# Moving transposes, a row broadcast and additions of rows and diagonals from engines to DMA in a four-layer graph network kernel

## The chip, the cores and the metric

The kernel runs on one core of a Trainium2 chip. The metric is the device time in microseconds (us) of one execution of the whole kernel. The profile shows these engines: PE (TensorE, matrix products; PEld is its weight load), DVE (VectorE), ACT (ScalarE), POOL (GpSimd) and SP (SyncE, which issues DMA transfers). A matrix product in float32 shows as two passes in the profile, a transposition by TensorE as one.

## What is computed

32 independent graphs, each with 512 nodes of 256 features, go through four layers. Each layer aggregates over the graph's own 512x512 adjacency matrix, applies dense weights, adds its input and normalises each row (layer norm).

```python
# layer 0
h = (1.0 + eps) * x + einsum('bnm,bmd->bnd', adj, x)
x = layernorm(x + relu(h @ W1 + b1) @ W2 + b2)
# layer 1
h = einsum('bnm,bmo->bno', adj, x @ W.T + b)
x = layernorm(x + where(h > 0, h, alpha * h))
# layer 2
h = layer_norm(x, gamma, beta)
conv = einsum('bij,bjh->bih', adj, h) @ W_rel + b_rel + h @ W_root
x = layernorm(x + (x + relu(conv)))
# layer 3
h = (epsilon * x + einsum('bnm,bmd->bnd', adj, x)) @ W1 + b1
h = silu(h * rsqrt(mean(h * h, axis=-1) + 1e-6) * rms_weight)
x = layernorm(x + h @ W2 + b2)
```

The hidden width is 512 in layer 0 and 1024 in layer 3. All values are float32.

## The kernel before

*How the work is laid out.* A graph's features lie in a tile of 128 partitions (the nodes, in four chunks) by 4 x 256. Aggregation gives its result with features on the partitions and nodes along the row (`aT`), which is what the dense layers need. Large products are done by a scheme of seven products instead of eight (`seven`), so each has sums of blocks before it (`left_sums`, `right_sums`), done by VectorE, and sums of results after it (`take`, `put`). The sums of adjacency blocks are made once for each graph and used by all four layers.

*The self term.* Layers 0 and 3 add (1 + eps) x or epsilon x. The kernel adds a multiple of the identity (`loop0`, `loop3`, 128x128) to the diagonal blocks of the adjacency matrix and of two of its sums: four places (`self.loops`) of 2 x 128 columns. `sums` (line 650) copies the four blocks aside (`self.plain`, by two-dimensional DMA moves, `carry`), `with_loops` (671) writes block plus loop back with VectorE, and `restore` (667) moves the kept blocks back for layers 1 and 2.

*Bias rows.* `plus_row` (874) adds a 256-wide row to each of the four chunks of x in layers 0 and 3: four additions on GpSimd each time.

*Transposition in layer 2.* `layer2` (935) needs h with features on the partitions. It takes eight 128x128 transpositions on TensorE against an identity (`flip`, 477) into two PSUM banks and copies them to SBUF (lines 938 to 943).

*RMS factors in layer 3.* `column_sums` (793) adds the squares over the hidden width for each node; GpSimd raises to the power -0.5 (`inv_sqrt`, 513). The factor of each node must lie along the row on all 128 partitions, to multiply hT. Four `flip`s of the broadcast column write it to a PSUM bank `pr` (lines 975 to 977), and VectorE multiplies each of eight chunks by `pr` (981).

*What sets the order.* The kernel records every operation with its possible engines and assumed durations (`Plan.do`, `Plan.move`), then walks through them with a list planner (`Plan.order`, 317), which chooses an engine where two are allowed and writes out one fixed order for each engine. All 32 graphs are in this one list; up to `FLIGHT` = 4 are open at once, so that TensorE works on one graph while another waits. Each engine then runs its own list strictly in order. Since every operation is issued by two helper functions, the profile puts line 266 beside all computing and line 280 beside all DMA; groups are told apart by tile names: `room` is one of 36 work tiles of 128 x 1024, `few` one of 12 small ones, `ps` a PSUM bank, `A` a sum of weight blocks, `ident` the identity. All DMA is issued from SP.

```python
        pr = bank(N)
        for c in range(NC):
            flip(pr[:, c * P : (c + 1) * P], rstd[:, c : c + 1].spread(P, P))
```

Of the kernel before, what the change touches and what calls it, by code (L numbers as in the profile page):

```python
# [14 lines left out]
P = 128  # L15
Q = 32
# [10 lines left out]


def in_psum(x):
    return isinstance(x, Part) and x.room.pool.psum  # L30
# [35 lines left out]
def gpsimd_time(n):  # L66
    return 0.15 + n * 0.0024, 0.05


def power_time(n):  # L70
    return 0.37 + n * 0.158, 0.04
# [4 lines left out]
ISSUE, ADVANCE, AFTER, LANES = 0.45, 1.5, 0.35, 8  # L76
# [18 lines left out]
RULES = [(50, 2, last, near) for last in (12, 20) for near in (0, 0.5, 1)]  # L95


class Pool:


    def __init__(self, tiles, grain, spare, psum):
        self.tiles, self.grain, self.spare, self.psum = tiles, grain, spare, psum
        self.clear()

    def clear(self):
        self.rooms = [None] * len(self.tiles)

    def free(self):

        return sorted(  # L110
            (0.0 if r is None else r.until, i)
            for i, r in enumerate(self.rooms)
            if r is None or not r.left
        )


class Room:


    def __init__(self, pool):  # L120
        self.pool = pool
        self.uses = 0
        self.clear()

    def clear(self):
        self.index = None
        self.left = self.uses
        self.until = 0.0


class Part:
# [34 lines left out]
    def place(self):  # L166
        v = self.room.pool.tiles[self.room.index]
        for step in self.steps:
            v = step(v)
        return v  # L170
# [3 lines left out]
class Op:  # L174

    graph: int
    rank: tuple
    ways: dict  # L180
    port: set
    yields: bool
    kbytes: float
    rooms: list = field(default_factory=list)
# [6 lines left out]
class Plan:  # L191
# [10 lines left out]
    def grains(self, x):  # L202
        part = isinstance(x, Part)
        key, ap = (x.room, x.model) if part else (x.tensor.name, x)
        grain = x.room.pool.grain if part else P
        starts = [ap.offset % ap.ap[0][0]]
        dims = list(ap.ap)[1:]
        for step, n in dims[:-1]:
            starts = [s + step * i for s in starts for i in range(n)] if step else starts
        step, n = dims[-1]  # L210
        return {
            (key, g)
            for s in starts
            for g in range(s // grain, (s + step * (n - 1)) // grain + 1)
        }

    def add(self, ways, out, ins, ordered=None, port=(), kbytes=0):
        me = len(self.ops)
        op = Op(self.graph, (self.graph, me), ways, port, "scalar" in ways, kbytes)
        self.ops.append(op)  # L220
        before, results = set(), set()
        writes = self.grains(out) if out is not None else set()
# [22 lines left out]
    def do(self, out, *ways, ordered=None, scrap=None):  # L245
# [3 lines left out]
        port = set()  # L249
        for e, method, _, args, kw in ways:  # L250
            tiles = [x for x in (*args, *kw.values()) if isinstance(x, (bass.AP, Part))]
            ins += tiles
            if e == "gpsimd" and kw.get("op") != ALU.pow or e == "vector" and not (
                method.startswith("bn_") or any(in_psum(x) for x in tiles)
            ):
                port.add(e)

        def issue(engine, method, args, kw):
# [14 lines left out]
            out, ins, ordered, port,  # L273
        )

    def move(self, out, src, kbytes, inward=True):


        def issue():
            self.nc.sync.dma_start(*(x.place() if isinstance(x, Part) else x for x in (out, src)))  # L280

        self.add(
            {"sync": ((ISSUE, ADVANCE + wire_time(kbytes) + AFTER), issue)},
            out if inward else None, [src] if isinstance(src, Part) else [], kbytes=kbytes,
        )
# [31 lines left out]
    def order(self, period, pace, last, near):  # L317
# [15 lines left out]
        oldest, port, wire, lanes = 0, 0.0, 0.0, [0.0] * LANES  # L333
        can_start = {i for i, n in enumerate(behind) if not n}
        done = []
        while can_start:
# [4 lines left out]
            def rooms_free(op):  # L341

                count = {}
                for r in op.rooms:
                    if r.index is None:
                        count[r.pool] = count.get(r.pool, 0) + 1
                at = 0.0
                for pool, n in count.items():
                    if pool not in room_at:
                        room_at[pool] = pool.free()  # L350
                    n += pool.spare[min(op.graph - oldest, len(pool.spare) - 1)]
                    if op.graph - oldest >= self.flight or n > len(room_at[pool]):
                        return None
                    at = max(at, room_at[pool][n - 1][0])
                return at

            best = {}
            for i in can_start:
                op = self.ops[i]
                wait = rooms_free(op)  # L360
                if wait is None:
                    continue
                if op.kbytes:
                    wait = max(wait, lanes[0])
                at = {
                    e: max(free[e], wait, ready[i][e], port if e in op.port else 0.0)
                    for e in op.ways
                }
                way = min(at, key=lambda e: at[e] + sum(op.ways[e][0]) + (YIELD if op.yields and e == "vector" else 0.0))
                best.setdefault(way, []).append((at[way], rank[i], i))  # L370
# [10 lines left out]
            if op.kbytes:  # L381
                wire = max(wire, t + ADVANCE) + wire_time(op.kbytes)
                end = wire + AFTER
                lanes = [*lanes[1:], end]
            if engine in op.port:
                port = end
            for r in op.rooms:
                if r.index is None:
                    r.index = r.pool.free()[0][1]
                    r.pool.rooms[r.index] = r  # L390
# [16 lines left out]
def tile_gnn_stack(ctx: ExitStack, tc: tile.TileContext, a: dict, out: bass.AP):  # L407
# [36 lines left out]
    FLIGHT, ROOMS, SMALL = 4, 36, 12  # L444
# [3 lines left out]
    psum = ctx.enter_context(tc.tile_pool(name="psum", bufs=1, space=bass.MemoryType.PSUM))  # L448
    plan = Plan(nc, FLIGHT)

    def pool(kind, name, n, size, grain, spare):
        return Pool(
            [kind.tile([P, size], F32, tag=f"{name}{i}", name=f"{name}{i}") for i in range(n)],
            grain, spare, kind is psum,
# [3 lines left out]
    rooms = pool(work, "room", ROOMS, NC * D, P, (0, 4, 6, 8))  # L458
# [5 lines left out]

    def gpsimd(method, n, *args, **kw):
        return "gpsimd", method, gpsimd_time(n), args, kw
# [22 lines left out]
    def both(method, o, x, y, engines):  # L489
        plan.do(o, *(e(method, span(o), x, y) for e in engines))  # L490

    def add(o, x, y, *engines):
        both("tensor_add", o, x, y, engines or (vector,))

    def sub(o, x, y, *engines):
        both("tensor_sub", o, x, y, engines or (vector,))

    def mul(o, x, y):
        both("tensor_mul", o, x, y, (vector,))
# [10 lines left out]
    def carry(o, x):  # L510
        plan.move(o, x, P * span(o) / 256)

    def inv_sqrt(o, x):
        n = span(o)
        plan.do(
            o, ("gpsimd", "tensor_tensor", power_time(n), (x, mhalf[:, 0:n]), dict(op=ALU.pow))
# [3 lines left out]
    def room(*shape):  # L520
        return Part(Room(rooms)).shaped(*shape)

# [57 lines left out]
    nc.vector.memset(mhalf, -0.5)  # L580

# [52 lines left out]
    class Adjacency:  # L634
# [15 lines left out]
        def sums(self):  # L650
# [8 lines left out]
            kept = room(4, HC, P)  # L659
            self.plain = [kept[:, i] for i in range(4)]  # L660
            for d, o in zip(self.plain, self.loops):
                if plan.graph:
                    carry(d, o)
                else:
                    copy(d, o)

        def restore(self):
            for d, o in zip(self.plain, self.loops):
                carry(o, d)

        def with_loops(self, loop):
            for d, o in zip(self.plain, self.loops):
                add(o, d, loop.unsqueeze(1).to_broadcast(list(o.shape)), vector)

        def row_sums(self):

            rows = room(N)
# [79 lines left out]
    def dense_sums(upper, lower):  # L757
# [3 lines left out]
        for pairs in zip(upper, lower):  # L761
            blocks = [x[:, :, j * TH : (j + 1) * TH] for x in pairs for j in range(2)]
            sums = right_sums(*blocks, [room(2, TH) for _ in range(3)], blocks[1])
# [29 lines left out]
    def column_sums(t, put):  # L793
# [3 lines left out]
        few = small(16)  # L797
# [7 lines left out]
        for q in range(1, P // Q):  # L805
            add(few[0:Q], few[0:Q], few[q * Q : (q + 1) * Q])
        for q in range(P // Q):
            put(slice(q * Q, (q + 1) * Q), few[0:Q, q :: P // Q])
# [64 lines left out]

    def plus_row(x, r):

        for c in range(NC):
            add(x[:, c, :], x[:, c, :], r, gpsimd)
# [31 lines left out]
    def layer1(x, adjacency):  # L909
# [4 lines left out]
        column_sums(rows, lambda p, sums: ts(rs[p], sums, 1.0, None, ALU.mult))  # L914
# [20 lines left out]
    def layer2(h, xx, u, adjacency):  # L935

        aT = aggregate(h, adjacency)
        hT = Wide(DC)
        for j in range(DC):
            ps = bank(N)  # L940
            for c in range(NC):
                flip(ps[:, c * P : (c + 1) * P], h[:, c, j * P : (j + 1) * P])
            copy(hT.chunk(j), ps)
# [11 lines left out]
    def layer3(x, adjacency, b):  # L955
# [3 lines left out]
        hT, acc = Wide(FC3), room(N)  # L959
# [11 lines left out]
        few = small(2, NC)  # L971
        ve, rstd = few[:, 0, :], few[:, 1, :]
        column_sums(acc, lambda p, sums: ts(ve[p], sums, 1.0 / HID3, RMS_EPS, ALU.mult, ALU.add))
        inv_sqrt(rstd, ve)
        pr = bank(N)
        for c in range(NC):
            flip(pr[:, c * P : (c + 1) * P], rstd[:, c : c + 1].spread(P, P))
# [12 lines left out]
        plan.move(place, y, N * D / 256, inward=False)  # L990
# [95 lines left out]
```

## Time and profile before

| | |
|---|---|
| median of 3 runs | 2365.2 us (2365.17 to 2367.01) |
| the profiled execution, its own time | 2366.02 us |
| its span, first to last instruction | 2364.2 us |
| DMA moved | 107.25 MB, 14.5% of 16 engines' span on SP's queue |

The profile is of one execution. Busy times of PE are unions of records that overlap, so a mean duration is longer than the distance from one pass to the next. The groups that do most of the work:

```profile
L266 PE MATMUL ps<-room,room 128*128 128x256 f32 x3584 | 911.9, 380 | 9.8 <-DMA room<-in_x_dram 5.8
L266 PE MATMUL ps<-L_gnn_W,room 128*128 128x128 f32 (+1 forms) x3584 | 622.7, 291 | 7.2 <-ACT room L266 4.9
L266 POOL TENSOR_TENSOR room<-room,L_gnn_b 128x256 f32<-128x256 f32 x256 | 194.6, 769 | 739.6 <-PE ps L266 519.0
L266 POOL TENSOR_TENSOR few<-few,mhalf 128x4 f32<-128x4 f32 (+1 forms) x160 | 212.5, 1329 | 1211.0 <-DVE few L266 1208.5
room<-in_adj_dram SPq DMA_DIRECT2D x128, 256.0 KB, 5.0
room<-room SPq DMA_DIRECT2D x252, 128.0 KB, 2.2
out_dram<-room SPq DMA_DIRECT2D x32, 512.0 KB, 3.0
```

A computing line has the count after x, then the busy time in us and the mean of one in ns, then the idle time of the engine just before the group and what ended it. A transfer's line has the count, the size of one and the median us from issue to landing.

### The profile page before, as it was taken

What the parts mean: (1) busy time and instruction counts of PE and PEld (TensorE: products, weight loads), DVE (VectorE), ACT (ScalarE), POOL (GpSimd) and SP (SyncE); (2) the same over time, 40 slices, a digit from 0 to 9 for tenths busy, and PEclk for the clock granted to TensorE, in tenths of its full rate; (3) what the DMA queues carried; (4) which work ended last, traced back from release to release, by engine and by line L of the source; (5) the groups of instructions that cost most, each with busy time, mean ns of one, the idle gap of its engine ahead of it and who ended that gap; (6) DMA issues with size and microseconds to landing.
All of it is one profiled execution on the core that took longest, in us unless ns stands there. A gap on an engine that the chain in (4) does not pass through costs nothing.

```text
span 2364.2 us, 40948 instructions
## 1 busy us (share of the span) xinstructions
PE 2330.0 (99%) x14362; PEld 2135.4 (90%) x14362; DVE 2138.4 (90%) x5485; ACT 1570.1 (66%) x3994; POOL 407.7 (17%) x422
## 2 busy tenths in 40 slices
PE   8999999999999999999999999999999999989997
PEld 7899989999999999999999999999999989978997
DVE  6899989999999999999999999999999999988997
ACT  3767666667666676766676666776666766565764
POOL 1112111111121121111111211111111112111111
PEclk9999999999999999999999999999999999999999
DMA  7001110111110111101111101111011111011000
GB/s 218 12 8 54 50 54 12 52 50 51 53 35 30 50 54 50 54 14 50 50 52 52 44 20 50 54 50 54 14 50 50 52 52 46 23 52 48 10 10 28
DMA packets 103487, 107.25 MB, mean 45 GB/s; under 512 B 10865, under 2 KB 78193, under 8 KB 103281
## 3 DMA queue, kind: packets, MB, share of 16 engines
q1 hardware_dynamic: 103280, 104.64, 14.5%
q8 instruction: 113, 1.85, 0.3%
q14 instruction: 94, 0.76, 0.1%
HBM read 54.80 MB, written 16.78 MB: 30 GB/s over the span
## 4 chain that ended last, share of the span: by engine, by line
PE 91%; DVE 4%; DMA 2%; ACT 1%; issue 1%; SPq 0%; POOL 0%; POOLq 0%; ACTq 0%; DVEq 0%
PE ps L266 91%; DVE room L266 3%; ACT room L266 1%; DVE few L266 1%; DMA room<-in_x_dram 1%; ACT scrap L266 1%; DMA room<-room 1%; SPq L280 0%; DMA L_gnn_eps<-in_L_gnn_eps_dram 0%; DMA room<-in_adj_dram 0%; POOL few L266 0%; ACT L266 0%; POOLq L1082 0%; DVE L_gnn_W L266 0%; DVE A L266 0%
## 5 line engine op out<-in xcount | busy, mean ns | idle before, releaser
L266 PE MATMUL ps<-room,room 128*128 128x256 f32 x3584 | 911.9, 380 | 9.8 <-DMA room<-in_x_dram 5.8
L266 DVE TENSOR_TENSOR room<-ps,room 128x256 f32<-128x256 f32 (+1 forms) x1344 | 629.6, 475 | 149.3 <-PE ps L266 122.6
L266 PEld LDWEIGHTS ps<-room,room 128*128 128x128 f32 x3584 | 650.1, 191 | 88.8 <-issue 7.1
L266 DVE TENSOR_TENSOR room<-room,room 128x512 f32<-128x512 f32 (+1 forms) x1120 | 640.6, 585 | 9.9 <-ACT room L266 3.1
L266 PE MATMUL ps<-L_gnn_W,room 128*128 128x128 f32 (+1 forms) x3584 | 622.7, 291 | 7.2 <-ACT room L266 4.9
L266 PEld LDWEIGHTS ps<-L_gnn_W,room 128*128 128x128 f32 x3584 | 525.3, 192 | 31.1 <-ACT room L266 7.2
L266 PE MATMUL ps<-A,room 128*128 128x128 f32 x3072 | 489.2, 276 | 1.8 <-ACT room L266 1.1
L266 PEld LDWEIGHTS ps<-A,room 128*128 128x128 f32 x3072 | 434.8, 192 | 15.8 <-ACT room L266 1.3
L266 PE MATMUL ps<-room,L_gnn_W 128*128 128x256 f32 x1536 | 424.6, 380 | 1.0 <-DVE room L266 0.9
L266 ACT ACTIVATE room<-ps,L_gnn_b_c 128x256 f32<-128x256 f32 x768 | 318.2, 472 | 157.2 <-PE ps L266 157.0
L266 POOL TENSOR_TENSOR few<-few,mhalf 128x4 f32<-128x4 f32 (+1 forms) x160 | 212.5, 1329 | 1211.0 <-DVE few L266 1208.5
L266 ACT ACTIVATE room<-ps 128x256 f32<-128x256 f32 (+1 forms) x546 | 215.0, 407 | 298.5 <-PE ps L266 294.7
L266 ACT ACTIVATE room<-room,few 128x256 f32<-128x256 f32 x624 | 341.0, 603 | 107.0 <-DVE few L266 103.7
L266 DVE TENSOR_TENSOR room<-room 128x256 f32<-128x256 f32 (+1 forms) x640 | 330.4, 518 | 18.0 <-DMA room<-in_adj_dram 5.7
L266 POOL TENSOR_TENSOR room<-room,L_gnn_b 128x256 f32<-128x256 f32 x256 | 194.6, 769 | 739.6 <-PE ps L266 519.0
L266 PE MATMUL ps<-room,A 128*128 128x256 f32 x1152 | 319.2, 380 | 3.0 <-ACT room L266 3.0
L266 PEld LDWEIGHTS ps<-room,L_gnn_W 128*128 128x128 f32 x1536 | 279.7, 191 | 33.1 <-DVE room L266 2.2
L266 ACT ACTIVATE room<-room 128x1024 f32<-128x1024 f32 (+2 forms) x260 | 245.8, 946 | 18.1 <-DVE room L266 16.5
L266 ACT ACTIVATE room<-room,L_gnn_rms_weight_c 128x512 f32<-128x512 f32 x256 | 179.7, 718 | 111.3 <-DVE room L266 108.2
L266 PEld LDWEIGHTS ps<-room,A 128*128 128x128 f32 x1152 | 206.5, 191 | 27.1 <-ACT room L266 4.2
L266 ACT ACTIVATE scrap<-room 128x256 f32<-128x256 f32 x384 | 157.2, 411 | 74.3 <-DVE room L266 63.1
L266 ACT ACTIVATE scrap<-room,few 128x256 f32<-128x256 f32 x384 | 190.7, 498 | 18.1 <-DVE few L266 16.3
(53 smaller groups left out, 1453.4 us busy)
## 6 DMA issues: line engine op xcount, KB each, us to landing
room<-in_adj_dram SPq DMA_DIRECT2D x128, 256.0 KB, 5.0
room<-room SPq DMA_DIRECT2D x252, 128.0 KB, 2.2
room<-in_x_dram SPq DMA_DIRECT2D x32, 512.0 KB, 6.0
out_dram<-room SPq DMA_DIRECT2D x32, 512.0 KB, 3.0
L_gnn_W<-in_L_gnn_W_dram SPq DMA_DIRECT2D x2, 1024.0 KB, 8.5
L_gnn_W<-in_L_gnn_W_dram SPq DMA_DIRECT2D x2, 512.0 KB, 8.1
L_gnn_b<-in_L_gnn_b_dram SPq DMA_DIRECT2D x3, 128.0 KB, 5.0
L_gnn_W_rel<-in_L_gnn_W_rel_dram SPq DMA_DIRECT2D x1, 256.0 KB, 7.2
```

The source lines that it names most:

```text
L266: getattr(getattr(self.nc, engine), method)(to, *(put(x) for x in args), **kw)
```

## The change

For the 30 middle graphs (the first and the last, `alone()`, keep the old ways):

- *Transposition:* VectorE transposes the 32x32 blocks of h in two instructions of 128x512; sixteen DMA moves from SP put the blocks in their places, in runs of 128 bytes.
- *RMS factors:* four small copies and a 32x32 transpose on VectorE arrange the factors; a DMA writes them as 16 rows of 128 bytes to a line in DRAM, and another reads the line back to all 128 partitions. VectorE multiplies by that SBUF tile.
- *Bias rows and loops:* `pour` issues an accumulating DMA from GpSimd that adds to its destination: one for each bias row (512 KB), four for each set of loops.
- *Keeping and restoring:* two blocks are kept in DRAM; the other two, parts of the adjacency matrix itself, are loaded again from the input in four moves of 64 KB. The SBUF tile of the kept blocks is gone. Graph 0 keeps all four in SBUF.

Bias rows come from `pour` in all graphs. The planner changes as well: up to five graphs are open, 11 small tiles; a work tile can be given out in two halves (`short`); the assumed times of DMA (0.8 us after the wire instead of 0.35, 1.5 us issue on GpSimd) and of the power are others; dependences are tracked by groups of 32 partitions too; and two rules of priority are tried instead of six.

```diff
-ISSUE, ADVANCE, AFTER, LANES = 0.45, 1.5, 0.35, 8
+ISSUE, ADVANCE, AFTER, LANES = dict(sync=0.45, gpsimd=1.5), 1.5, 0.8, 8
-RULES = [(50, 2, last, near) for last in (12, 20) for near in (0, 0.5, 1)]
+RULES = [(36, 2, last, 0.5) for last in (12, 20)]
...
-    FLIGHT, ROOMS, SMALL = 4, 36, 12
+    FLIGHT, ROOMS, SMALL = 5, 36, 11
...
-    rooms = pool(work, "room", ROOMS, NC * D, P, (0, 4, 6, 8))
+    rooms = pool(work, "room", ROOMS, NC * D, P, (0, 2, 4, 4))
...
+    def alone():
+        return plan.graph in (0, B - 1)
...
+    def pour(o, x):
+        plan.move(
+            o, x, 2 * P * span(o) / 256, "gpsimd", late=1.0, outof=(o, x), accum_op=ALU.add
+        )
...
+            if plan.graph:
+                self.kept = next(diagonals)
+                for i in (2, 3):
+                    d = self.kept[:, i - 2]
+                    name = f"{self.kept.tensor.name}{i}"
+                    plan.move(d, self.loops[i], P * HC * P / 256, into=name)
+            else:
+                self.kept = room(4, HC, P)
+                for i in range(4):
+                    copy(self.kept[:, i], self.loops[i])
+
+        def restore(self):
+            for i in range(4):
+                if plan.graph == 0:
+                    carry(self.loops[i], self.kept[:, i])
+                elif i < 2:
+                    for k in range(HC):
+                        c = i * HC + k
+                        block = a["adj"][plan.graph][:, c, c * P : (c + 1) * P]
+                        plan.move(self.loops[i][:, k], block, P * P / 256)
                 else:
-                    copy(d, o)
+                    name = f"{self.kept.tensor.name}{i}"
+                    d = self.kept[:, i - 2]
+                    plan.move(self.loops[i], d, P * HC * P / 256, outof=[name])
...
         def with_loops(self, loop):
-            for d, o in zip(self.plain, self.loops):
-                add(o, d, loop.unsqueeze(1).to_broadcast(list(o.shape)), vector)
+            for o in self.loops:
+                loops = loop.unsqueeze(1).to_broadcast(list(o.shape))
+                if alone():
+                    add(o, o, loops)
+                else:
+                    pour(o, loops)
...
+    def turned(h):
+        hT = Wide(DC)
+        if alone():
+            for k in range(DC):
+                ps = bank(N)
+                for c in range(NC):
+                    flip(ps[:, c * P : (c + 1) * P], h[:, c, k * P : (k + 1) * P])
+                copy(hT.chunk(k), ps)
+        else:
+            squares = Wide(DC)
+            for k in range(DC):
+                o = squares.chunk(k)
+                plan.do(o, vector("transpose", N, h[:, :, k * P : (k + 1) * P]))
+            places = [slice(q * Q, (q + 1) * Q) for q in range(P // Q)]
+            to, of = (
+                x.pair(0).then(lambda v: v.rearrange("p k (c i) -> p (k c) i", i=P))
+                for x in (hT, squares)
+            )
+            for p in places:
+                for q in places:
+                    carry(to[p, :, q], of[q, :, p])
+        return hT
+
+    def everywhere(sums, ops):
+        few = small(2, NC)
+        ve, power = few[:, 0, :], few[:, 1, :]
+        by_token(ve, sums, *ops)
+        inv_sqrt(power, ve)
+        if alone():
+            o = bank(N)
+            for c in range(NC):
+                flip(o[:, c * P : (c + 1) * P], power[:, c : c + 1].spread(P, P))
+        else:
+            few = small(2, Q)
+            square, turned = few[0:Q, 0, :], few[0:Q, 1, :]
+            for q in range(P // Q):
+                ts(square[:, q : N // Q : P // Q], power[q * Q : (q + 1) * Q], 1.0, None, ALU.mult)
+            plan.do(turned, vector("transpose", Q, square))
+            o, line = short(N), next(lines)
+            name = line.tensor.name
+            plan.move(line.rearrange("(m i) -> m i", i=Q), turned[0 : N // Q], N / 256, into=name)
+            plan.move(o, line.partition_broadcast(P), P * N / 256, late=0.8, outof=[name])
+        return o
+
     def plus_row(x, r):
-        for c in range(NC):
-            add(x[:, c, :], x[:, c, :], r, gpsimd)
+        pour(x, r.unsqueeze(1).to_broadcast([P, NC, D]))
```

## The prediction

> **What bounds the kernel now.** I read the page's shares first, then busy time by stretch, then TensorE's waits, then the chain that ended last. Shares and chain:
>
> ```profile
> PE 2330.0 (99%) x14362; PEld 2135.4 (90%) x14362; DVE 2138.4 (90%) x5485; ACT 1570.1 (66%) x3994; POOL 407.7 (17%) x422
> PE 91%; DVE 4%; DMA 2%; ACT 1%; issue 1%; SPq 0%; POOL 0%; POOLq 0%; ACTq 0%; DVEq 0%
> ```
>
> An average of 99% hides stages, so busy time by stretch decides (columns: length, then busy time and count for PE, PEld, DVE, ACT, POOL, then clock, DMA share, GB/s):
>
> ```profile
> 0.00:60.00 60.00, 51.89 (x239) 43.85 (x240) 41.68 (x112) 22.43 (x57) 7.51 (x15) 0.97 0.71 215
> 60.00:120.00 60.00, 56.86 (x317) 50.73 (x316) 53.34 (x139) 43.57 (x126) 11.78 (x12) 1.00 0.05 14
> 600.00:1000.00 400.00, 400.00 (x2440) 366.94 (x2439) 367.88 (x945) 274.38 (x696) 71.54 (x72) 1.00 0.16 47
> 1000.00:1400.00 400.00, 400.00 (x2525) 369.64 (x2525) 369.06 (x946) 267.49 (x685) 70.01 (x71) 1.00 0.14 42
> 1400.00:1800.00 400.00, 400.00 (x2464) 367.63 (x2463) 368.10 (x939) 277.90 (x699) 71.46 (x72) 1.00 0.16 48
> 2100.00:2200.00 100.00, 95.61 (x574) 85.70 (x573) 84.02 (x216) 61.09 (x169) 19.74 (x22) 1.00 0.12 35
> 2340.00:2365.00 25.00, 14.87 (x112) 14.39 (x112) 15.03 (x39) 8.72 (x15) 2.01 (x2) 0.80 0.11 43
> ```
>
> From 600 to 1800 us TensorE has no gap at all. VectorE follows with 92%. Idle time exists only while the first graphs load and while the last drain. The output transfers give the period: 72.09 us for one graph.
>
> ```profile
> 1064.32 0.35 SPq L280 DMA_DIRECT2D out_dram<-room  x1
> 1136.41 0.35 SPq L280 DMA_DIRECT2D out_dram<-room  x1
> ```
>
> So a pass taken off TensorE shortens the run by its pitch, for as long as nothing else becomes late. The pitch is read where passes follow one another (start, length, operation), since durations overlap:
>
> ```profile
> 134.44 0.67 PE L266 MATMUL ps<-room,L_gnn_W 128*128 128x256 f32 x2
> 134.94 0.60 PE L266 MATMUL ps<-ident,few 128*128 128x128 f32 x4
> 135.38 0.60 PE L266 MATMUL ps<-room,L_gnn_W 128*128 128x256 f32 x2
> 135.81 0.39 PE L266 MATMUL ps<-A,room 128*128 128x128 f32 x2
> ```
>
> Four flips take 135.38 - 134.94 = 0.44 us, 0.11 each, not the 273 ns of one record. A product of 256 columns is two passes and takes 0.43.
>
> [...] a power of 4 columns takes 1243 ns on average and 1.01 us in the quiet tail.
>
> **The change, part by part.** The rows it touches (count, busy time, mean ns of one):
>
> ```profile
> L266 PE MATMUL ps<-ident,room 128*128 128x128 f32 x256 | 48.7, 273 | 0.0
> L266 PE MATMUL ps<-ident,few 128*128 128x128 f32 x128 | 19.7, 274 | 1.9 <-POOL few L266 1.9
> L266 DVE TENSOR_TENSOR room<-room,loop 128x256 f32<-128x256 f32 x256 | 103.9, 416 | 3.1 <-DMA room<-room 2.4 <-PE ps L266 0.2
> L266 DVE TRANSPOSE_TENSOR_REDUCE few<-room 128x16 f32<-128x512 f32 x64 | 45.2, 707 | 0.9
> ```
>
> *TensorE.* 256 + 128 flips are 12 a graph. Graphs 0 and 31 keep theirs, so 30 x 12 x 0.11 = 39.6 us go; at a finer pitch of 0.109, 39.2. All of it is on the bound. The built program agrees: 360 TensorE instructions fewer.
>
> *VectorE, each middle graph.* Away: eight loop adds, 8 x 0.416 = 3.33. Added: two transposes of 128x512, priced by the 707 ns row, 1.41 (from 1.2, the pitch of a plain 512-column addition, to 2.0); four strided copies and a 32x32 transpose at 0.16, 0.81; the RMS products read SBUF and not PSUM, 8 x (696 - 679 ns) = 0.14. Sum -0.97. Its load goes from 92% of 72.1 to about 65.3 of 70.8, again 92%. It does not become the bound. ScalarE loses two copies of 597 ns and has room.
>
> *GpSimd.* Away: eight row adds of 769 ns, 6.15. Left: five powers, 4 x 1.24 + 1.67 = 6.6. Added: ten accumulating transfers. Their issue cost is in no row. The new constants assume 1.5 us; below I ask how much is bearable. At 1.5 the engine is 21.6 us of 70.8 busy.
>
> *SP.* 14 transfers become 32: 16 for the transpose, 2 for the line, 2 more for restoring, 2 instead of 4 kept. The old 128 KB moves (256 runs, as the new ones) take a median of 0.594 us on the queue and 2.2 to land, so the sixteen take 15 x 0.594 + 2.2 = 11.1 us. All 32 take some 18 us of 70.8. DMA was 14.5% busy; it has room.
>
> *Distances.* With no cover the new chains would cost their length; cover is the work of the other graphs. I counted, in the built order of a middle graph, the TensorE work between what releases a chain and the first product that needs it. Transpose: needs 1.4 + 11.1 + some 1.5 of sums, has 29. Restoring: has over 40. The RMS line: two 128 KB-class trips and a diagonal restore ahead of it on SP; from the restore's release it needs 0.6 + 3.2 to 5.0 (the loads' range) + 0.70 + 0.72, at most 7.1, and has 8.9. Loop block: this is the tightest. Four transfers stand in a row on GpSimd, the last being waited for 9.3 us after the first is released; a power stands behind them. With issue cost c and landing L it needs 3c + L. L lies between 2.2 (such a move from SP) and 5.0 (the median adjacency load); I take 4[...]. [...] I take the constant 1.5. That makes 8.5: 0.8 to spare.
>
> *Start and end.* Before, TensorE loses about 16 us in the first 120 and 21 after 1900. The fifth graph in flight and the half buffers loosen the order: links with under 1.6 us of cover fall from 74 to 62 in the last four hundreds of microseconds of the order and from 39 to 32 in the first 100. But the transposes have only 12 us at two places there, against 11.1 + 1.4. I take -4 us, with -12 and +8 as ends.
>
> Sum: the profiled execution took 2366.0 (span 2364.2 and 1.8 around it), 0.8 above the median. 2366.0 - 39.3 - 4 = 2322.7; against the median 2322. I say 2323.
>
> **Rivals.**
> *A, full gain (0.72):* 2311 to 2336 by the ends above.
> *B, part of the gain lost (0.11):* a chain on GpSimd or the line is late by 0.3 to 1.0 us every graph, 30 x that = 9 to 30 us: 2332 to 2353. For it: margins of 0.8 and 1.8 us. Against: POOL is 30% busy, so it recovers before the next graph.
> *C, slower (0.12):* GpSimd's issue cost. TensorE in order has no slack, so what the loop block is late is lost in each of 30 graphs. With L = 4, 3c + L passes 9.3 at c = 1.77 and the saved 1.31 us is gone at 3c + L = 10.6, c = 2.2. At c = 3 the block is 3.7 us late: 30 x (3.7 - 1.31) = 72 us slower, 2437. [...] Against: c must be near four times the 0.594 us that SP takes for as many.
> *D, nothing gained (0.05):* VectorE, at 92%, takes over because its transpose or its sums wait for buffers; at 100% of 65.3 the period could not exceed 70.8, so it needs 6 to 7 us more a graph that no row shows: 2361 to 2369.
>
> **How the numbers follow.** Within 0.2% (4.7 us) counts as no change. Faster: A, nearly all of B, a share of D, 0.84. Same 0.05. Slower 0.11 (C less what falls just under the bound). The range reaches from 2309 to 2350: A whole and most of B.
>
> **What would show it.** Right: a period of 70.8 us between outputs, TensorE at 400 of 400 in the middle, flips x16 and x8. Wrong: waits of TensorE on DMA into `room` that come every 71 us, or a median issue over 2 us on POOL (C); waits on VectorE in the middle (D); a middle as forecast with longer ends would refute only my -4.

## The result and the profile after

The changed kernel takes 2485.4 us (median of 4 runs, 2481.1 to 2495.1), against 2365.8 us before: a ratio of 1.051, 95% interval 1.048 to 1.054. It is 120 us slower. The profiled execution took 2495.1 us with a span of 2493.3.

Shares of the span, and the chain that ended last by engine, from the page of the changed kernel:

```profile
PE 2373.0 (95%) x14002; PEld 2129.0 (85%) x14002; DVE 2075.9 (83%) x5478; ACT 1533.5 (62%) x3922; POOL 596.5 (24%) x470
PE 50%; DVE 28%; SPq 12%; DMA 4%; issue 3%; ACT 2%; DVEq 0%; POOLq 0%; ACTq 0%
```

The 360 passes are gone from TensorE. Yet its busy time has grown by 43 us, and its idle time from 34 to 120 us. VectorE is less busy than before, not more. The share "SPq" is new: the time in which the end waited for SP to issue transfers.

Busy time by stretch, the columns as before the change (the column after POOL is TensorE's granted clock):

```profile
600.00:1000.00 400.00, 384.81 (x2277) 344.85 (x2276) 335.90 (x901) 249.27 (x641) 102.72 (x81) 0.98 0.41 75
1000.00:1400.00 400.00, 382.93 (x2264) 343.02 (x2263) 334.73 (x885) 254.65 (x654) 101.58 (x79) 0.98 0.40 76
1400.00:1800.00 400.00, 380.79 (x2227) 341.07 (x2226) 327.25 (x861) 247.51 (x627) 100.13 (x77) 0.96 0.39 74
```

The loss lies in the middle, where TensorE had no gap before. Now it has 15 to 19 us of gaps in 400, and its clock is granted to 96 to 98% instead of 100%.

From the waits of the changed kernel, TensorE's longest and VectorE's for transfers from tile to tile (total us, times, longest):

```profile
PE ps L284 <- DVE room L284: 95.3, 66, 4.2
DVE room L284 <- DMA room<-room: 83.7, 27, 4.7
PE ps L284 <- ACT room L284: 7.5, 8, 1.9
```

TensorE waits for VectorE, and VectorE waits 27 times for a DMA from tile to tile: once in nearly every middle graph. Only the transposing moves have that name in the middle graphs.

One such place, from the timeline of the changed kernel (start, length, engine, operation, count, and the idle time before it):

```profile
1013.98 2.61 POOL L284 TENSOR_TENSOR few<-few,mhalf 128x8 f32<-128x8 f32 x1 [9.16 <-ACT room L284]
1016.82 2.07 ACT L284 ACTIVATE room<-room,few 128x256 f32<-128x256 f32 x4 [0.35 <-DVE few L284]
1020.03 1.29 DVE L284 STREAM_TRANSPOSE room<-room 128x512 f32<-128x512 f32 x2
1021.40 12.41 SPq L299 DMA_DIRECT2D room<-room  x16
1035.18 0.69 DVE L284 TENSOR_TENSOR room<-room 128x512 f32<-128x512 f32 x1 [2.98 <-DMA room<-room]
1039.10 0.41 DVE L284 TENSOR_TENSOR room<-ps,room 128x256 f32<-128x256 f32 x1
1039.57 1.16 PE L284 MATMUL ps<-A,room 128*128 128x128 f32 x8 [3.02 <-DVE room L284]
```

Read it downwards. The two transposes on VectorE take 1.29 us, near the 1.41 forecast. Then SP needs 12.41 us to issue the sixteen moves, 0.78 us each; the planner had assumed 0.45, or 7.2 us for all. The first sum over the transposed h stands ready in VectorE's fixed order and holds everything behind it for 2.98 us. TensorE then stops for 3.02 us.

The clock adds to it. A longer stop of the same kernel, with what follows it:

```profile
1342.12 0.38 PE L284 MATMUL ps<-A,room 128*128 128x128 f32 x2
1346.35 2.08 PE L284 MATMUL ps<-A,room 128*128 128x128 f32 x8 [3.85 <-DVE room L284]
```

```profile
1345.00:1352.00 7.00, 5.65 (x19) 4.99 (x20) 1.72 (x5) 0.38 (x1) 0.28 (x1) 0.52 0.86 263
1352.00:1362.00 10.00, 10.00 (x64) 9.23 (x63) 5.19 (x11) 5.19 (x13) 0.91 (x1) 1.00 0.12 13
```

After the stop of 3.85 us the same eight passes take 2.08 us that took 1.16 after the stop of 3.02: the granted clock was 0.52 from 1345 to 1352, and 1.00 from 1036 to 1046. Over the span the mean clock is 0.975, against 0.997 before. The clock record of the trace has 27 spells at half clock, 126 us in all. TensorE had passes running in 109 of them, so some 54 us of work were lost, against 3 before.

So the difference of the spans, 129 us, is made of 86 us more idle time of TensorE, 51 us more at half clock, 39 us less for the flips, and some 31 us that remain: passes spaced wider than usual without recorded idle time. The run with half of the moves, below, still has such a remainder: 2320.3 us of busy time, where 2330.0 - 39.3 = 2290.7 would do.

### The profile page after: what moved, and what is told of

Read it like the earlier page. It is cut to its first block, busy times and chain, and to the rows that moved or that the text cites. A ratio compares the mean times of both kernels' runs of the same rounds, so it can differ in the third digit from the quotient of the medians.

```text
span 2493.3 us, 41603 instructions
## 1 busy us (share of the span) xinstructions
PE 2373.0 (95%) x14002; PEld 2129.0 (85%) x14002; DVE 2075.9 (83%) x5478; ACT 1533.5 (62%) x3922; POOL 596.5 (24%) x470
## 4 chain that ended last, share of the span: by engine, by line
PE 50%; DVE 28%; SPq 12%; DMA 4%; issue 3%; ACT 2%; DVEq 0%; POOLq 0%; ACTq 0%
PE ps L284 50%; DVE room L284 24%; SPq L299 12%; DVE few L284 4%; DMA room<-room 2%; ACT room L284 2%; ACT scrap L284 1%; DMA room<-in_adj_dram 1%; DMA L_gnn_eps<-in_L_gnn_eps_dram 0%; DMA room<-in_x_dram 0%; DMA L_gnn_alpha<-in_L_gnn_alpha_dram 0%; DMA room<-diagonal 0%; DVE A L284 0%; DVEq L284 0%; DVE L_gnn_W L284 0%
## 5 line engine op out<-in xcount | busy, mean ns | idle before, releaser
L284 PE MATMUL ps<-room,room 128*128 128x256 f32 x3584 | 957.0, 388 | 21.2 <-DVE room L284 15.7
L284 DVE TENSOR_TENSOR room<-ps,room 128x256 f32<-128x256 f32 (+1 forms) x1344 | 612.1, 472 | 249.3 <-PE ps L284 236.8
L284 DVE TENSOR_TENSOR room<-room,room 128x512 f32<-128x512 f32 (+1 forms) x1360 | 774.6, 593 | 11.3 <-ACT room L284 4.2
L284 PE MATMUL ps<-L_gnn_W,room 128*128 128x128 f32 (+1 forms) x3584 | 607.2, 293 | 4.6 <-ACT room L284 2.5
L284 PEld LDWEIGHTS ps<-L_gnn_W,room 128*128 128x128 f32 x3584 | 523.4, 192 | 70.8 <-DVE room L284 30.3
L284 PEld LDWEIGHTS ps<-A,room 128*128 128x128 f32 x3072 | 458.3, 198 | 107.4 <-DVE room L284 79.4
L299 POOL DMA_DIRECT2D room<-loop x240 | 319.3, 1593 | 960.0 <-PE ps L284 880.6
L284 POOL TENSOR_TENSOR few<-few,mhalf 128x4 f32<-128x4 f32 (+1 forms) x160 | 245.5, 1535 | 773.4 <-DVE few L284 574.5
L284 ACT ACTIVATE room<-room,few 128x256 f32<-128x256 f32 x584 | 303.2, 591 | 146.0 <-DVE few L284 145.7
L284 DVE TENSOR_TENSOR room<-room 128x256 f32<-128x256 f32 (+1 forms) x640 | 307.8, 495 | 99.5 <-DMA room<-room 83.7
L284 ACT ACTIVATE room<-ps 128x256 f32<-128x256 f32 (+1 forms) x514 | 190.9, 379 | 278.9 <-PE ps L284 274.8
```

The costliest lines, as they stand in the source:

```text
L284: getattr(getattr(self.nc, engine), method)(to, *(put(x) for x in args), **kw)
L299: getattr(self.nc, engine).dma_start(to, of, **kw)
```

## The experiments

Three theories were held against one another. T: the sixteen moves occupy SP for 12 us where the fixed order leaves room for 7; TensorE stops for it, and its clock with it. G: what GpSimd does, accumulating transfers and powers, comes late. S came up after the first runs: small VectorE instructions take longer than planned. Every altered kernel but three (half of the moves, no accumulating transfers, SP 0.78) also has another rule of priority in the planner, and so another order on all engines. Such a run compares two whole orders, not one constant alone. The table has the medians; the ratio is to the kernel before, with its interval.

| run | us | ratio |
|---|---|---|
| changed kernel | 2485.4 | 1.051 (1.048 to 1.054) |
| half of the moves left out, same order | 2361.6 | 0.998 (0.998 to 0.999) |
| no accumulating transfers, same order | 2403.8 | 1.016 (1.014 to 1.018) |
| SP 0.62 | 2375.1 | 1.004 (1.003 to 1.006) |
| SP 0.78 | 2390.5 | 1.011 (1.009 to 1.012) |
| transposition of h back on TensorE | 2395.3 | 1.013 (1.011 to 1.015) |
| VectorE floor 0.16 alone | 2448.5 | 1.035 (1.032 to 1.038) |
| SP 0.62 and floor 0.16 | 2330.2 | 0.987 (0.984 to 0.989) |
| the same, all flips back on TensorE | 2353.5 | 0.995 (0.993 to 0.996) |
| the same, RMS flips back on TensorE | 2364.9 | 1.000 (0.999 to 1.002) |
| SP 0.70 and floor 0.16 | 2323.7 | 0.983 (0.981 to 0.984) |
| SP 0.62, floor 0.16, loops on VectorE | 2314.8 | 0.979 (0.978 to 0.981) |
| SP 0.70, floor 0.16, loops on VectorE | 2320.2 | 0.981 (0.979 to 0.983) |

**Half of the moves left out.** The order on every engine is that of the changed kernel; only the issue of every second move is dropped, so half of h's blocks don't reach their places.

```diff
-                for q in places:
-                    carry(to[p, :, q], of[q, :, p])
+            for n, (p, q) in enumerate((p, q) for p in places for q in places):
+                carry(to[p, :, q], of[q, :, p], left_out=n % 2)
```

> The changed kernel in exactly its order on every engine, but every second of the sixteen transposing moves is not issued (half of the transposed h is then not brought to its place). T: the burst takes about 6 us, under the 7.2 the order allows, so the regular stop is gone: 2318 to 2340 us. G: the stop stays, 2440 to 2490 us.

It took 2361.6 us, 124 less than the changed kernel. SP's burst, TensorE's waits and the middle of this run:

```profile
1045.10 6.43 SPq L301 DMA_DIRECT2D room<-room  x8
```

```profile
PE ps L284 <- DVE room L284: 15.3, 43, 1.7
```

```profile
1000.00:1400.00 400.00, 398.75 (x2410) 357.74 (x2408) 357.43 (x954) 267.98 (x693) 111.51 (x87) 1.00 0.40 76
```

The burst fits, the regular stop is gone, the clock is granted in full (1.00), while GpSimd does all that it did. So the regular stop needs the length of the burst; lateness on GpSimd alone, as G has it, doesn't make it. But the time is 22 us above the top of what T expected: the outputs of this run are 72.26 us apart, not 70.8:

```profile
1057.07 0.35 SPq L301 DMA_DIRECT2D out_dram<-room  x1
1129.33 0.35 SPq L301 DMA_DIRECT2D out_dram<-room  x1
```

VectorE's timeline of this run shows where the planned order slips (no idle time is noted before any of these; those that start before another's end overlap):

```profile
1013.45 0.16 DVE L284 TENSOR_TENSOR few<-few 32x16 f32<-32x16 f32 x1
1013.64 0.43 DVE L284 TENSOR_TENSOR room<-room,room 128x256 f32<-128x256 f32 x1
1014.08 0.16 DVE L284 TENSOR_TENSOR few<-few 32x16 f32<-32x16 f32 x1
1015.53 0.67 DVE L284 TENSOR_SCALAR few<-few 32x4 f32<-32x4 f32 x4
1016.57 0.16 DVE L284 TENSOR_SCALAR few<-few 128x2 f32<-128x2 f32 x1
1016.63 0.42 DVE L284 TENSOR_TENSOR room<-room 128x256 f32<-128x256 f32 x1
1019.23 0.67 DVE L284 TENSOR_SCALAR few<-few 32x4 f32<-32x4 f32 x4
```

Four instructions on 32 partitions take 0.67 us, 0.17 each; the planner has 0.06 for each. The instruction on 128 partitions at 1016.57 lets its follower start after 0.06 and does fit. Three additions and four scalings were there before; the new way of spreading the RMS factors adds four more and a transpose to the same stretch, in which VectorE has no gap. Eleven instructions at 0.11 us each would make 1.2 of the 1.46 us between 70.8 and 72.26. That is an estimate; no run takes these instructions away and changes nothing else. Why these four are 0.17 us apart, and the follower at 1016.63 only 0.06 behind, was not shown.

**No accumulating transfers.** `pour` issues nothing; the order is unchanged.

> The changed kernel in exactly its order, but no accumulating transfer is issued from GpSimd (bias rows and loops are not added in any graph but those of the first and last that add loops on VectorE). T: the sixteen moves still take SP 0.61 us each, 10 us or more against 7.2, so a stop of 1 to 3 us a graph stays: 2380 to 2470 us. G: all of it goes, 2318 to 2340 us.

It took 2403.8 us, as T expected. The burst and the waits of this run:

```profile
1131.66 10.40 SPq L301 DMA_DIRECT2D room<-room  x16
```

```profile
PE ps L284 <- DVE room L284: 48.3, 61, 2.6
```

Without GpSimd's transfers most of the moves take about 0.6 us, and the sixteen still pass the 7.2 us of the order, so TensorE still stops. With them some moves take 1.2 to 1.4 us. So the stop doesn't come from the accumulating transfers, but 82 of the 120 us go with them. The traces show how: over the thirty graphs the burst takes 12.3 us on average with them and 10.8 without, while its first move comes equally soon after the adjacency loads that SP issues before it (14.29 us after 1007.11 in the changed kernel, 14.26 after 1117.40 here). TensorE's idle time falls by 46 us and the work lost at half clock from 54 to 7 us; together that is nearly all of the 94 us between the two spans.

**The planner told 0.62 us, and 0.78 us, for an issue from SP.** One constant is changed; with 0.62 the old rule of priority gives no order at all, so another was taken.

```diff
-ISSUE, ADVANCE, AFTER, LANES = dict(sync=0.45, gpsimd=1.5), 1.5, 0.8, 8
+ISSUE, ADVANCE, AFTER, LANES = dict(sync=0.62, gpsimd=1.5), 1.5, 0.8, 8
-RULES = [(36, 2, last, 0.5) for last in (12, 20)]
+RULES = [(36, 2, 12, 0)]
```

> The changed kernel with one assumption of its planner altered: a transfer issued from SP occupies SP for 0.62 us, not 0.45 (most of the sixteen transposing moves took 0.61 in its trace); no plan comes out with the old rule of priority, so near is 0 instead of 0.5. Theory T (the burst of sixteen moves takes SP 12 us where the order was laid out for 7, so transposed h comes late and TensorE stops once a graph): the stop shrinks from some 3 us to under 1, 2315 to 2345 us. Rival G (accumulating transfers and powers on GpSimd are what comes late): the order still rests on the same GpSimd times, 2450 to 2490 us.

> The same with 0.78 us for an issue from SP, the mean over the burst in the trace (12.4 us / 16), and the changed kernel's own rule of priority (near 0.5). T: no regular stop is left, 2318 to 2340 us. G: 2450 to 2490 us.

2375.1 and 2390.5 us: both did far better than G allowed, and both missed what T had promised, by 30 and 51 us. The burst itself is as long as ever, in the run with 0.62:

```profile
1055.59 12.50 SPq L299 DMA_DIRECT2D room<-room  x16
```

```profile
PE ps L284 <- DVE room L284: 34.8, 67, 3.0
```

The burst has not changed; the order now leaves it more room. The run with 0.78 shows that a longer assumption alone is not better: its outputs come irregularly. Why that order is worse wasn't looked into.

**Only the transposition of h back on TensorE.**

> The changed kernel with its own assumptions, but the transposition of h stays on TensorE in all graphs (no sixteen moves); the old rule gives no plan, so near is 0. T: no stop of several us is left and the TensorE clock is granted in full; S stays at up to 1.5 us a graph: 2345 to 2390 us. G (accumulating transfers are late): 2440 to 2490 us.

2395.3 us, 5 above the range that T and S gave, and far below G. Its clock is granted in full in the middle (1.00); waits of TensorE for VectorE sum to 20.2 us, none over 1.3.

**A floor of 0.16 us for VectorE's instructions**, alone and with 0.62 for SP:

```diff
-    return 0.06 + n * 0.00106, 0.085
+    return max(0.16, 0.06 + n * 0.00106), 0.085
```

> Only the floor of 0.16 us for VectorE instructions; SP's issue stays assumed at 0.45; rule of priority 36, 1. T: the stop behind the sixteen moves stays, 2390 to 2490 us. If S were the whole cause: 2318 to 2342 us.

> Both assumptions altered: 0.62 us for an issue from SP, and at least 0.16 us for any VectorE instruction (the small ones on 4 to 16 columns are planned at 0.06 to 0.08, and take 0.16 to 0.17 each [...]); rule of priority 38, 0.25. With T and S (small VectorE work [...] costs 1.5 us a graph where VectorE has no gap, as the half-carries run left it): no regular loss stays, period near 71 us, 2318 to 2342 us. Without S: as with 0.62 alone, 2360 to 2385 us.

Alone 2448.5 us: the floor without room for the burst changes little, and the stops stay (89.2 us of waits for VectorE). Together 2330.2 us, 155 less than the changed kernel, with every operation of the change in place. The middle of that run:

```profile
1000.00:1400.00 400.00, 399.84 (x2427) 365.22 (x2426) 368.66 (x966) 264.69 (x695) 102.29 (x80) 1.00 0.42 79
```

```profile
1045.32 0.35 SPq L299 DMA_DIRECT2D out_dram<-room  x1
1116.49 0.35 SPq L299 DMA_DIRECT2D out_dram<-room  x1
```

A period of 71.17 us, with TensorE nearly full. An order laid out with both durations thus loses almost nothing of what was lost. How much of the 45 us between this run and the one with 0.62 alone is S, and how much the other rule of priority, no run separates.

**What the flips are worth**, with both assumptions set:

> Both assumptions altered as in the run with both, but the transposition of h and the spreading of the RMS factors are back on TensorE in all graphs; accumulating transfers, restoring from DRAM and five graphs in flight stay. If TensorE is the bound in both, this is 12 x 0.11 x 30 = 39 us slower than the run with both: 2350 to 2380 us. If transfers or VectorE bound the other, the two differ by less than 20 us.

> Both assumptions altered (0.62 us, 0.16 us), and the RMS factors spread by TensorE in all graphs, without the line in DRAM and its five small VectorE instructions (rule of priority 38, 0.25). TensorE has 4 x 0.11 x 30 = 13 us more to do; if TensorE alone bounds, 2338 to 2352 us; if the line's small VectorE work is what the run with both still loses, 2322 to 2337 us.

With all flips back 2353.5 us, 23 us slower than the run it is compared with, not 39. That run lost 0.4 to 1.0 us a graph, while the order with the flips back is full in the middle (400.00 of 400 us). Its outputs are 72.09 us apart, exactly as in the kernel before:

```profile
1022.78 0.35 SPq L299 DMA_DIRECT2D out_dram<-room  x1
1094.87 0.35 SPq L299 DMA_DIRECT2D out_dram<-room  x1
```

So its middle is that of the kernel before, with the same passes on TensorE, and the 12 us by which it is faster lie at the start and the end. With the RMS flips alone back, 2364.9 us missed both ranges; TensorE waits 23.9 us for VectorE in that order, and the cause wasn't found.

**Towards a better version:** 0.70 for SP, loops on VectorE, and both.

```diff
-                if alone():
+                if True:
                     add(o, o, loops)
```

> As the run with both assumptions altered, with 0.70 us instead of 0.62 for an issue from SP (rule of priority 38, 0), to allow for the moves that take 1.2 to 1.4 us beside GpSimd's transfers. If what that run still loses (0.4 to 1.0 us a graph) comes from those moves, 2312 to 2328 us; if not, 2325 to 2345 us.

> Both assumptions altered (0.62 us, 0.16 us), and the loops added by VectorE in place in all graphs, not by accumulating transfers (rule of priority 38, 0.5). T says that these transfers only slow some of SP's moves: 2315 to 2340 us, no slower than the run with both by more than 10 us. If taking loops off VectorE were worth what VectorE saves, 8 x 0.33 us a graph, it is 40 to 80 us slower: 2370 to 2410 us.

> The two best altered kernels joined: 0.70 us for an issue from SP, the floor of 0.16 us for VectorE, loops added by VectorE in all graphs; rule of priority 40, 0.25. The middle graphs already take 70.8 us in both parents, so only start and end can gain: 2305 to 2320 us. If the parents' gains came from the middle and add, 2295 to 2305 us.

2323.7, 2314.8 and 2320.2 us. The best is the one with the loops back on VectorE: 2.1% faster than the kernel before (ratio 0.979, 0.978 to 0.981). Its middle:

```profile
600.00:1000.00 400.00, 400.00 (x2476) 369.44 (x2475) 375.16 (x1001) 265.95 (x688) 51.94 (x39) 1.00 0.29 68
```

VectorE is at 94% here and TensorE loses nothing. The outputs of this order show what the flips are worth where TensorE is full in both:

```profile
963.31 0.35 SPq L299 DMA_DIRECT2D out_dram<-room  x1
1034.13 0.35 SPq L299 DMA_DIRECT2D out_dram<-room  x1
```

The period is 70.82 us against the 72.09 with the flips on TensorE: 1.27 us a graph for twelve flips, 0.106 each, or 38 us over 30 graphs. Joining the two changes gained nothing more.

## Why the prediction was wrong

*What bounds the kernel, and what a flip is worth:* right. In the orders that fit the measured durations the middle is full, and the period of 70.82 us is the 70.8 forecast. That the run with 0.70 took 2323.7 us where 2323 was forecast is partly luck: start and end gave some 12 us in the run with all flips back, not 4, and with 39 for the flips that makes 2314, which the run with the loops on VectorE reached (2314.8).

*The distance of the transposition* is the step that failed: "needs 1.4 + 11.1 + some 1.5 of sums, has 29". Both sides were wrong.
- What it has: 29 us were counted from the last pass of TensorE that releases the chain. Between that pass and the first move stand the sums, a power and the scaling of the layer norm, which were not counted (the power took 2.61 us and the scaling 2.07 in the place shown), and the two transposes of h, which were. From the first move, at 1021.40, TensorE's product was due at 1039.57 - 3.02 = 1036.55: 15.2 us.
- What it needs: from 1021.40 to the landing before 1035.18 are 13.8 us, not 11.1, since some moves take over 1 us beside GpSimd's transfers (1.40, 1.23 and 1.19 in this burst); then VectorE takes 1039.10 + 0.41 - 1035.18 = 4.3 us, not 1.5, since it works in order and other instructions stand in between. Together 18.1, some 3 too many.

The evidence was in hand: the old moves showed 0.594 us on SP, the forecast itself used that figure, and the diff has 0.45 for the order. The forecast set its 11.1 us against the 29 and not against the 7.2 that the order had laid out.

*The side that would be slower* was put in the wrong place. Rival C had the right form, a late chain whose whole delay is lost in each graph, but on GpSimd. Its issue took 1.59 us and landing 3.7, close to the 1.5 and 4 taken, and TensorE shows no wait for the loop transfers. Of the signs listed, waits on VectorE in the middle came, which stood for D; but VectorE itself was waiting for SP's moves.

*The size of the loss* exceeded even that rival, since a stop could cost twice: the granted clock was 0.52 around the end of the stop of 3.85 us and in the 5 us after it. No step considered the clock, though the stretches of before showed it: 0.97 and 0.80 in the two where TensorE had the most idle time, 8.1 us of 60 and 10.1 of 25. The length of a stop alone doesn't tell: the clock was 1.00 after one of 3.02 us and fell at shorter ones, as the last section shows.

*VectorE's sum*, -0.97 us a graph and no bound, was right in its sign as an average (2138 us fell to 2076, twice as far as forecast) and wrong as a conclusion. Rival D asked for 6 to 7 us more a graph over the whole period. In the run with half of the moves, 1.4 us more a graph were enough to lose the saving of 1.3, most likely in the stretch where VectorE has no gap. The 0.81 for the new small instructions was well priced; what was wrong was that it lay beside other work.

*Start and end:* the -4 us could not be seen in the changed kernel, where the order slipped. The run with all flips back shows 12 us there, at the far end of the range given. The stretches of before have 11.3 us of TensorE's gaps in the first 120 us, not 16, and the ends given for rival A reach from 2314 to 2335, not from 2311 to 2336; neither matters for the miss.

## What to carry to other kernels

In a kernel with a fixed order, the assumed durations are part of the program: a move assumed at 0.45 us that takes 0.61 or more is a small error once, but sixteen in a row took 12 us where the order had 7, and that stopped the bound engine. Compare the assumed cost of each repeated issue with the profile, and measure the cover of a chain from the moment its first instruction can start, not from the last pass of the bound engine. Where TensorE is full, a stop of 2 us or more should be counted with the half clock that can come with it, as it did here at 24 of the 27 stops of more than 1.9 us.

## What the runs showed of the hardware beyond that

Beside accumulating transfers some other work took longer. Some of SP's issues of 32 KB took 1.2 to 1.4 us, where the median of all was 0.61. The power of four columns on GpSimd had a mean of 1334 ns with them and 1109 without. The power of eight columns, 1672 ns in the kernel before, rose too, but not because of them: it is as long in the run without accumulating transfers (second line). What lengthened it stays open.

```profile
L284 POOL TENSOR_TENSOR few<-few,mhalf 128x8 f32<-128x8 f32 x32 | 74.9, 2340 | 265.7 <-ACT room L284 198.4 <-DVE few L284 66.7 <-PE ps L284 0.6
L284 POOL TENSOR_TENSOR few<-few,mhalf 128x8 f32<-128x8 f32 x32 | 74.3, 2322 | 398.3 <-ACT room L284 245.4 <-DVE few L284 153.0
```

The clock dropped at stops shorter than that of 3.02 us too: around one of 2.13 us, the mean clock of the stretch was 0.76.

```profile
2187.93 2.37 PE L284 MATMUL ps<-L_gnn_W_root,room 128*128 128x128 f32 x10 [2.13 <-DMA room<-room]
2185.00:2192.00 7.00, 4.87 (x27) 4.50 (x26) 4.98 (x16) 5.13 (x20) 0.96 (x2) 0.76 0.29 33
```

In the changed kernel's clock record the clock fell at 24 of the 27 stops of more than 1.9 us, at the latest 1.5 us after their end; the three without a drop lasted 2.49, 2.49 and 3.02 us. Apart from the last one at the end of the span, every spell at half clock lasted 3.41 or 6.83 us.
